# Handing out the y blocks of the second half in four parts a unit instead of one

## The chip, the cores and the metric

The kernel runs on one NeuronCore of a Trainium2 chip. The metric is the device time of one execution in microseconds (us), the median of several runs; less is better.

## The reference, cut to what matters

The reference has two layers on a 256 x 256 image of 128 channels. Layer 0 is a row attention (until about 1,655 us of the span). Layer 1 is a Fourier-operator block over 256 tokens (one token is a 256 x 128 plane): an attention whose value and projection are spectral convolutions, then two mixing layers, each a skip plus a spectral convolution over groups of four tokens, with instance norms. Cut to the part that the change touches:

```python
attn = fno_layer(attn, p_wr, p_wi, p_bias, p_sw, p_sb, (H, W))       # "y": attention-weighted tokens plus spectral image
attn = instance_norm(attn + tokens, attn_norm_w, attn_norm_b)
h0 = instance_norm(attn, norm2_w, norm2_b)                            # its statistics need all of y of those tokens
h1 = fno_layer(h0, mix_wr[0], mix_wi[0], ..., norm=True, act=True)    # first mixing layer: modes, then images
h2 = fno_layer(h1, mix_wr[1], mix_wi[1], ..., norm=True)              # second mixing layer
out = instance_norm(h2, mon_w, mon_b) + attn
```

The 256 tokens are worked on in two halves of 128 (half 0 and half 1)[...]. All data are float32.

## The kernel before

**Units of y.** `y_blocks(a, psum, lo, hi)` makes y of half `a` in units of 1,024 pixels, 32 units in all. A unit takes four PSUM banks (`yps`, one for each row residue `j`). For each `j`, TensorE adds two products of 128 x 256 (line 1351, over the two halves of the source tokens). After that come the products of `image` (line 1219, eight of 32 x 128 rows with the modes `gs`). Then VectorE writes the four banks out with a factor (line 1361, "eviction" below) and takes statistics of them (two `bn_stats`, line 1363). For half 1 the unit goes back to DRAM by a DMA that GpSimd issues (line 1365, tile `yt`, two buffers). The loads of unit `u + 2` (`xt`, three buffers, two DMAs of 512 KB on SyncE's queue, line 1017, and for every second unit four of `gs`, line 1248) are issued at the start of unit `u`.

**Banks.** PSUM is split between two sets of four banks, `bq` (tag q) and `br` (tag r). The units of half 1 use `br`, so a unit takes all of its set: the first product of the next unit waits for the eviction of the first bank.

**The mode chain of half 0.** While half 1's y is made, `first_modes(0)` works on the modes of the first mixing layer of half 0. Its steps are:

- `bn_aggr` of y's statistics (line 1451), then two chains of tiny VectorE operations, each with a square root on ScalarE (`rsqrt`, lines 35 to 43), that end in the tile `dg`;
- `rhops`, one product on TensorE (line 1468), its copy and the scaling of the modes `F` (lines 1471 to 1474);
- `mix_modes`: sixteen products `x0m` of 128 x 512 elements by VectorE or, every third one, GpSimd (line 1387, two buffers), each added into one of two banks by TensorE (`x0acc`, line 1400, identity as weights, 128 x 512). They are called step 0 to step 15 below;
- `mixed`: the copies and squares of the two banks (`x0Z`, `x0sq`, lines 1410 to 1416);
- four chunks of `synth_modes` (`g10gp`, 64 products each on TensorE, line 609; copies `g10gt`, line 617; DMAs `Gd`, line 622), and between them `norm`: the sums `x0ens` (line 1425), a third chain with a square root, then `x0rsp` (line 1438) and, after a product of it on VectorE (`bl`, line 1490), lines 1493 to 1508.

**Order.** The stages run in a `manual_schedule`: on every engine, SyncE included, instructions stand in the order in which the Python generators issue them, and each engine's queue is worked off in that order. `weave(main, side)` sets the order of the two chains. `main` yields a weight `t` after each of its steps. `weave` then takes parts of `side` until their own weights make up for it:

```python
for t in main:
    due += t
    while due > 0 and side is not None:
        u = next(side, None)
        ...
        due -= u
```

`y_blocks` yields 4.2 after each unit, so steps of the mode chain stand only between whole units. There are two such weaves: units 0 to 23 of half 1 with `first_modes(0)` (all of it), and units 24 to 31 with the first three yields of `second_modes(0)` (`f1ps` of its first two chunks, line 1629). Half 0 of y and the ends of both loops are run with `run`, which ignores the weights.

Of the kernel before, what the change touches and what calls it, by code (L numbers as in the profile page):

```python
# [22 lines left out]
def bc(ap, axis, n):  # L23

    a = ap.unsqueeze(axis)
    shape = list(a.shape)
    shape[axis] = n
    return a.to_broadcast(shape)
# [517 lines left out]
def layer1(tc, I, C, ident, x1d, upool, U, stats2, groups, out):  # L546
# [9 lines left out]
    with ExitStack() as ctx:  # L556
# [456 lines left out]
        def load_x1(a, u):  # L1013

            t = xp.tile([P, 2, NB // 2], FP, tag="xt", name=f"xt_{a}_{u}", bufs=3)
            for sc in range(2):
                nc.sync.dma_start(t[:, sc], x1v[:, sc, u * NB // 2 : (u + 1) * NB // 2])
            return t
# [188 lines left out]
        def by_turn(t):  # L1207

            return t.rearrange("p (n j w) -> p j n w", j=4, w=W)

        def rows_of(ps):
            return ps.rearrange("p (n w) -> p n w", w=W)

        def image(ps, gs, bs, rows=range(4)):

            for k, n in enumerate(rows):
                for j in range(4):
                    q = slice(32 * j, 32 * j + 32)
                    nc.tensor.matmul(  # L1219
                        ps[j][:, k * W : (k + 1) * W], gs[q, n, :], bs[q, :],  # L1220
                        start=False, stop=(k == len(rows) - 1),
                    )
# [16 lines left out]
        def load_modes(gs, Gd, b, tt=None):  # L1239
            for j in range(4):  # L1240
                q = slice(32 * j, 32 * j + 32)
                if tt is None:
                    nc.sync.dma_start(  # L1243
                        gs[q].rearrange("f n t -> f (n t)"),
                        Gd[:, j, 4 * b : 4 * b + 4, :].rearrange("f n t -> f (n t)"),
                    )
                else:
                    nc.sync.dma_start(gs[q], Gd[:, j, 4 * b : 4 * b + 4, tt])
# [78 lines left out]
        def y_blocks(a, psum, lo, hi, kept=16):  # L1327

            tt = slice(a * P, (a + 1) * P)
            gs = {}  # L1330

            def load(u):
                if (a, u) not in xts:
                    xts[a, u] = load_x1(a, u)
                if u % 2 == 0:
                    gs[u // 2] = xp.tile([P, 4, P], FP, tag="gs", name=f"gs_{a}_{u}", bufs=3)
                    load_modes(gs[u // 2], Gd0, u // 2, tt)

            load(lo)
            load(lo + 1)  # L1340
            yield 0.0
            for u in range(lo, hi):
                b, s = u // 2, u % 2
                if u + 2 < hi:
                    load(u + 2)
                xt = xts.pop((a, u))
                ps = [psum.pool.tile([P, 512], FP, tag=psum.tag, name=f"yps_{a}_{u}_{j}") for j in range(4)]
                ps = [z[:, 0:256] for z in ps]
                for j in range(4):
                    for sc in range(2):  # L1350
                        nc.tensor.matmul(  # L1351
                            rows_of(ps[j]), mpT[:, sc, tt], by_turn(xt[:, sc])[:, j],
                            start=(sc == 0), stop=False,
                        )
                image(ps, gs[b], bsy, range(2 * s, 2 * s + 2))
                if a == 0:
                    yt = blocks[:, b, s * HB : (s + 1) * HB]
                else:
                    yt = xp.tile([P, HB], FP, tag="yt", name=f"yt_{u}")
                for j in range(4):  # L1360
                    nc.vector.tensor_tensor(by_turn(yt)[:, j], rows_of(ps[j]), bc(rwb, 1, 2), ALU.mult)  # L1361
                for g in range(2):
                    nc.vector.bn_stats(ystat[:, a, 2 * u + g, :], yt[:, g * 512 : (g + 1) * 512])
                if a:
                    nc.gpsimd.dma_start(ydv[:, a, u * HB : (u + 1) * HB], yt)  # L1365
                yield 4.2

        def mix_modes(mk, acc, F, l, tag, cs):

# [443 lines left out]
        with tc.manual_schedule(engines=COMPUTE | {ENG.SP}):  # L1813
            with tc.tile_pool(name="psy", bufs=8, space=PSUM) as psy:
                run(y_blocks(0, Banks(psy, "y"), 0, 32))
# [6 lines left out]
            with yctx:  # L1822
                U1 = 24
                with tc.tile_pool(name="mp0", bufs=1) as wp:
                    y1 = y_blocks(1, br, 0, U1)
                    weave((2.4 * t for t in first_modes(0, wp, tiles(wp), bq, [(wp, "gt", 1)])), y1)
                    run(y1)
                with tc.tile_pool(name="hp0", bufs=2) as wp:
                    run(first_images(0, wp, xp, bq, br))
                with tc.tile_pool(name="mp1", bufs=1) as wp:  # L1830
                    y1 = y_blocks(1, br, U1, 32)
                    next(y1)
                    m0 = second_modes(
                        0, wp, tiles(wp), bq, [(xp, "xt", 3)], [(wp, "gt", 1)] * 3 + [(xp, "xt", 3)]
                    )
                    weave((2.4 * next(m0) for _ in range(3)), y1)
                    run(y1)
                    m1 = first_modes(
                        1, wp, Tiles(F=(xp, "yt", 2), f=(xp, "yt", 2), m=(xp, "gs", 3)), br, [(xp, "xt", 3)]
                    )  # L1840
                    next(m1)
                    for k, _ in enumerate(iter(lambda: next(m0), None)):
                        if k % 4 == 3:
                            next(m1)
                    for _ in m0:
                        next(m1, None)
                    o0 = output_0(bq)
                    next(o0)
                    y2 = wp.tile([P, NB], FP, tag="gt", name="y2_0", bufs=1)
                    nc.sync.dma_start(y2, ydv[:, 1, 0:NB])  # L1850
                    run(m1)
                    g2 = wp.tile([P, 4, P], FP, tag="m", name="gs2_1_0", bufs=2)
                    next(o0)
                    load_modes(g2, halves[1].Gd1, 0)
                    next(o0)
# [200 lines left out]
```

## Time and profile before

| | |
|---|---|
| time before, median of 3 runs | 2884.54 us (2880.02 to 2887.79) |
| profiled execution, its own time | 2878.79 us |
| its span, first to last instruction | 2877.0 us |
| TensorE (PE) busy in the span | 2643.1 us (92%) |
| VectorE (DVE) busy | 2004.2 us (70%) |
| units 0 to 23 of half 1, with `first_modes(0)` | about 2032 to 2190 us |
| of which `x0acc` and units 5 to 10 | about 2058 to 2110 us |
| units 24 to 31 of half 1 | about 2331 to 2385 us |

Times inside the profile are microseconds from the span's start. In the answers of the trace, a row of the timeline gives the start, the length, engine, line and operation, and in square brackets how long the engine was idle before it and what it waited for. A table of stretches gives the busy time in each, then the granted TensorE clock (1.00 is full), the share of the DMA engines and GB/s. TensorE runs each float32 product as two instructions, so a unit's eight products of line 1351 are 16 in the trace, and sixteen steps of `x0acc` are 32.

### The profile page before, as it was taken

Reading aid. Unit: us, or ns where it says so; the run is one execution under the profiler, and the core shown is the slowest. Engines: PE = TensorE matmul, PEld = TensorE weight load, DVE = VectorE, ACT = ScalarE, POOL = GpSimd, SP = SyncE. Lnnn points to the kernel's source line nnn. Section 1 sums busy time; section 2 is a strip of 40 time slices with the busy share of each in tenths; the row PEclk is TensorE's granted clock in tenths of the full one; section 3 lists DMA queues with packets and bytes.
Section 4 is the critical chain, followed back from the end, with each engine's and each line's share of the span. In section 5 each row is a group of like instructions: output and inputs, shape, how many; then the busy total and the mean of one; then the engine's idle time right before and its main releaser. Section 6 shows DMA issues by size and latency. Waiting matters only on the chain. (4 is left out here: it accounts for less than half of the span.)

```text
span 2877.0 us, 71481 instructions
## 1 busy us (share of the span) xinstructions
PE 2643.1 (92%) x29116; PEld 1935.1 (67%) x29116; DVE 2004.2 (70%) x3264; ACT 1488.4 (52%) x2847; POOL 1679.6 (58%) x1308
## 2 busy tenths in 40 slices
PE   7799999999999999999999989999889988799655
PEld 6677777777777777777777656778665555455533
DVE  7788888888888888888888854756645555365445
ACT  0477777777777777777777622200004611365132
POOL 0399999999999999999999900200114733111211
PEclk9999999999999999999999999999999999799865
DMA  9422222222222222222222101188879984798599
GB/s 369 166 67 67 67 67 67 67 67 67 68 67 67 67 67 67 67 67 67 67 67 67 47 22 54 34 276 274 281 243 312 311 304 134 253 363 306 187 360 339
DMA packets 246705, 430.12 MB, mean 149 GB/s; under 512 B 26278, under 2 KB 174201, under 8 KB 239976
## 3 DMA queue, kind: packets, MB, share of 16 engines
q1 hardware_dynamic: 206568, 335.34, 35.4%
q0 software_dynamic: 22912, 81.80, 7.4%
q10 hardware_dynamic: 16896, 8.39, 1.0%
q8 instruction: 231, 3.78, 0.6%
q14 instruction: 98, 0.80, 0.1%
HBM read 290.17 MB, written 135.27 MB: 148 GB/s over the span
## 5 line engine op out<-in xcount | busy, mean ns | idle before, releaser
L332 POOL TENSOR_TENSOR e<-e,b1T 128x1024 f32<-128x1024 f32 x256 | 606.1, 2367 | 164.6 <-PE u L381 90.3
L336 POOL TENSOR_TENSOR es<-e 128x512 f32<-128x512 f32 x512 | 639.6, 1270 | 20.1
L314 ACT ACTIVATE sc<-sc,b2T 128x512 f32<-128x512 f32 x512 | 339.0, 662 | 364.6 <-PE sc L305 356.2
L356 DVE RECIPROCAL av<-av 128x256 f32<-128x256 f32 x256 | 452.3, 1767 | 27.2 <-DVE og L355 1.4
L314 ACT ACTIVATE e<-sc,b2T 128x512 f32<-128x512 f32 x512 | 348.6, 681 | 0.0
L327 DVE TENSOR_TENSOR e<-sc,b1T 128x1024 f32<-128x1024 f32 x256 | 311.0, 1215 | 0.0
L305 PE MATMUL sc<-qkT 32*128 32x256 f32 x4096 | 293.4, 400 | 1.3 <-DVE e L327 1.3
L344 PE MATMUL av<-e,v 128*32 128x256 f32 x4096 | 274.7, 385 | 0.5 <-POOL e L332 0.5
L305 PEld LDWEIGHTS sc<-qkT 32*128 32x128 f32 x4096 | 185.1, 184 | 112.2 <-issue 97.7
L1351 PE MATMUL yps<-xt,mpT 128*128 128x256 f32 x1024 | 241.8, 389 | 19.4 <-DVE yt L1361 9.7
L355 DVE SCALAR_TENSOR_TENSOR og<-gate,av 128x256 f32<-128x256 f32 x256 | 107.7, 421 | 190.6 <-PE av L349 190.6
L1351 PEld LDWEIGHTS yps<-xt,mpT 128*128 128x128 f32 x1024 | 191.9, 192 | 56.7 <-DVE yt L1361 13.0
L1365 POOL DMA_DIRECT2D yd<-yt x32 | 17.7, 555 | 340.8 <-DVE yt L1361 340.8
L360 POOL TENSOR_TENSOR x<-xt,bo 128x256 f32<-128x256 f32 x256 | 187.7, 734 | 0.0
L279 PE MATMUL qk<-xnT,wT_wq 128*128 128x256 f32 x512 | 179.5, 432 | 1.7 <-ACT xnT L271 1.7
L285 PEld LDWEIGHTS gv<-wT_wv,kvT 128*128 128x128 f32 x1024 | 155.0, 192 | 13.3
L349 PE MATMUL av<-es,ones 128*32 128x256 f32 x2048 | 157.5, 379 | 2.5 <-POOL es L336 2.5
L366 PE MATMUL wo<-wT_wo,og 128*128 128x128 f32 x1024 | 156.8, 276 | 2.7 <-DVE og L357 2.7
L344 PEld LDWEIGHTS av<-e,v 128*32 128x32 f32 x4096 | 107.0, 109 | 76.1 <-POOL e L332 1.0
L381 PE MATMUL u<-adft,x 128*128 128x129 f32 x1024 | 156.4, 275 | 0.0
L285 PE MATMUL gv<-wT_wv,kvT 128*128 128x128 f32 x1024 | 156.0, 275 | 0.0
L1718 ACT ACTIVATE blocks<-h2ps,col 128x512 f32<-128x512 f32 x128 | 89.0, 779 | 129.4 <-PE h2ps L1219 129.4
(546 smaller groups left out, 5282.8 us busy)
## 6 DMA issues: line engine op xcount, KB each, us to landing
xt<-x1d SPq DMA_DIRECT2D x128, 512.0 KB, 5.9
xb<-in_x_dram SPq DMA_DIRECT2D x32, 1024.0 KB, 7.8
xt<-in_x_dram SPq DMA_DIRECT2D x128, 256.0 KB, 2.7
kt<-in_L_conv_kv_x_dram SPq DMA_DIRECT2D x128, 256.0 KB
x1d<-x SPq DMA_DIRECT2D x256, 128.0 KB, 2.3
y<-yd SPq DMA_DIRECT2D x62, 512.0 KB, 8.9
gs<-Gd SPq DMA_DIRECT2D x384, 64.0 KB, 5.1
yd<-yt POOLq DMA_DIRECT2D x32, 512.0 KB, 6.3
```

The costliest lines, as they stand in the source:

```text
L279: nc.tensor.matmul(ps[:, 0:256], wT["wq"], xnT, start=True, stop=True)
L285: nc.tensor.matmul(ps[:, 256 + c * P : 256 + (c + 1) * P], kvT[:, c * P : (c + 1) * P], wT["wv"], start=True, stop=True,)
L305: nc.tensor.matmul(sc[h // 2][:, h % 2, c * 256 : (c + 1) * 256], qkT[p, 256 + c * P : 256 + (c + 1) * P], qkT[p, 0:256], start=True, stop ...
L314: nc.scalar.activation(r["e"][1][:, :, c, :] if hp else z, z, AF.Exp, bias=b2T[:, c, s : s + 1])
L327: nc.vector.tensor_tensor(r["e"][0].rearrange("p h c q -> p (h c q)"), r.pop("sc").rearrange("p h x -> p (h x)"), b1T[:, 0:2].rearrange("p ...
L332: nc.gpsimd.tensor_tensor(e1, e1, b1T[:, 2:4].rearrange("p h c q -> p (h c q)"), ALU.mult)
L336: nc.gpsimd.tensor_tensor(r["es"][hp], e[:, :, 0, :], e[:, :, 1, :], ALU.add)
L344: nc.tensor.matmul(ps[hd, 0:256], r["v"][:, c, hd], r["e"][h // 2][:, h % 2, c, :], start=(c == 0), stop=(c == 1),)
L349: nc.tensor.matmul(ps[32 * h : 32 * h + 32, 256:512], self.ones, r["es"][h // 2][:, h % 2, :], start=True, stop=True,)
L356: nc.vector.reciprocal(rd, rd)
L360: nc.gpsimd.tensor_tensor(r["x1"], r["x"], bc(self.bo, 1, 2), ALU.add)
L1351: nc.tensor.matmul(rows_of(ps[j]), mpT[:, sc, tt], by_turn(xt[:, sc])[:, j], start=(sc == 0), stop=False,)
```

## The change

A unit of y now yields three more times, after the products of `j` = 0, 1 and 2, with 0.86 each, and 1.62 instead of 4.2 at its end; the sum is the same. The generator's own instructions and their order among themselves do not change, nor do buffers or banks. In the two weaves, steps of the mode chain can now stand after each pair of products of a unit.

```diff
--- before.py
+++ after.py
@@ -1352,6 +1352,8 @@
                             rows_of(ps[j]), mpT[:, sc, tt], by_turn(xt[:, sc])[:, j],
                             start=(sc == 0), stop=False,
                         )
+                    if j < 3:
+                        yield 0.86
                 image(ps, gs[b], bsy, range(2 * s, 2 * s + 2))
                 if a == 0:
                     yt = blocks[:, b, s * HB : (s + 1) * HB]
@@ -1363,7 +1365,7 @@
                     nc.vector.bn_stats(ystat[:, a, 2 * u + g, :], yt[:, g * 512 : (g + 1) * 512])
                 if a:
                     nc.gpsimd.dma_start(ydv[:, a, u * HB : (u + 1) * HB], yt)
-                yield 4.2
+                yield 1.62
 
         def mix_modes(mk, acc, F, l, tag, cs):
```

In the order of the two built programs, these instructions of the mode chains change place (unit numbers are of half 1; a step of `x0acc` on TensorE, its product `x0m` on VectorE or GpSimd):

| what | before | after |
|---|---|---|
| first chain with a square root (VectorE) | after the eviction of unit 0 | ahead of it |
| second chain (VectorE) | after the eviction of unit 1 | ahead of it |
| `rhops` (TensorE) | after unit 3 | in unit 3, after `j` = 0 |
| steps 0 and 1 of `x0acc` | after unit 5 | in unit 5, after `j` = 0 and `j` = 1 |
| step 2 | after unit 5 | after unit 5 |
| steps 3 to 14 | three after each of units 6 to 9 | in each of units 6 to 9 one after `j` = 0, one after `j` = 1 (unit 6) or `j` = 2 (7 to 9), one after the unit |
| step 15 | after unit 10 | in unit 10, after `j` = 0 |
| VectorE's copy `x0Z` | after the eviction of unit 10 | ahead of it |
| `x0ens` | after unit 12 | in unit 12, after `j` = 1 |
| `x0rsp`, lines 1493 to 1508, third `g10gp` | after unit 15 | in unit 15, after `j` = 1; on VectorE ahead of its eviction, on GpSimd ahead of its DMA |
| first `f1ps` of `second_modes(0)` | after unit 27 | in unit 27, after `j` = 2; its copy ahead of the eviction |

On SyncE's queue nothing changes place; half 0 of y is unchanged.

## The prediction

> **What bounds the stage now.** I read the page first for the whole (TensorE is busy 92% of the span), then the waits of TensorE between 2030 and 2170 us, where units 0 to 18 of half 1 run with the mode chain of half 0, then the timelines of TensorE, VectorE and GpSimd there, then tables of stretches for clock and DMA. The change moves no instruction outside half 1's two weaves, so the rest can only shift as a block.
>
> The waits of TensorE in that window:
> ```profile
> PE x0acc L1400 <- POOL x0m L1387: 7.7, 5, 1.6
> PE yps L1351 <- DVE yt L1361: 5.3, 8, 1.4
> PE g10gp L609 <- ACT x0sq L1416: 2.9, 1, 2.9
> PE x0rsp L1493 <- DVE bl L1490: 2.6, 1, 2.6
> ```
> The columns are us in total, times, longest. Five waits of 1.5 us are the third step of each group of three; two long single waits follow. TensorE's timeline shows one full period of such a unit (start, length, work; the idle before in brackets):
> ```profile
> 2070.68 1.98 PE L1400 MATMUL x0acc<-x0m,ident 128*128 128x512 f32 x4
> 2074.21 1.12 PE L1400 MATMUL x0acc<-x0m,ident 128*128 128x512 f32 x2 [1.55 <-POOL x0m L1387]
> 2075.17 3.62 PE L1351 MATMUL yps<-xt,mpT 128*128 128x256 f32 x16
> 2078.72 0.73 PE L1219 MATMUL yps<-bsy,gs 32*128 32x128 f32 x16
> 2079.38 1.98 PE L1400 MATMUL x0acc<-x0m,ident 128*128 128x512 f32 x4
> ```
> The period is 2079.38 - 2070.68 = 8.70 us. Start to start, products take 3.55, the image 0.66, a step 0.95; full work is 3.55 + 0.66 + 3 x 0.95 = 7.06. The reader should see that 1.6 us per unit is idle. Its cause is in VectorE's and GpSimd's timelines:
> ```profile
> 2070.77 1.42 DVE L1361 TENSOR_TENSOR yt<-yps,rwb 128x256 f32<-128x256 f32 x4 [3.40 <-PE yps L1219]
> 2072.22 1.28 DVE L1363 BATCH_NORM_STATS2 ystat<-yt 128x6 f32<-128x512 f32 x2
> 2073.42 1.29 DVE L1387 TENSOR_TENSOR x0m<-F,mixwi 128x512 f32<-128x512 f32 x1
> 2073.10 1.06 POOL L1387 TENSOR_TENSOR x0m<-F,mixwn 128x512 f32<-128x512 f32 x1
> ```
> GpSimd's product stands behind the DMA of `yt`, VectorE's behind eviction and statistics: 2.66 us from the start of an eviction to the next `x0m`.
>
> The clock, before, in and after the two long waits:
> ```profile
> 2101.30:2109.50 8.20, 5.30 (x35) 1.00 0.62 212
> 2109.50:2113.10 3.60, 3.56 (x128) 0.53 0.27 106
> 2142.70:2145.40 2.70, 2.32 (x12) 0.69 1.05 391
> 2145.40:2149.40 4.00, 4.00 (x130) 0.50 0.52 183
> 2149.40:2154.30 4.90, 4.90 (x41) 0.88 0.57 154
> ```
> The column after TensorE's busy time and count is the granted clock. A `g10gp` chunk takes 2.03 us at full clock (2128.41 to 2130.44) and 3.60 here.
>
> [...]after the waits of 1.43 to 1.55 us in this stage the clock stayed at 1.00, after 2.03 (at 2456 us), 2.19 (2194 and 2495), 2.36 (2406), 2.58 and 2.94 us it was 0.50 to 0.56; one wait of 2.72 (2725 us) went without. [...]`x0m` on VectorE takes 0.69 us alone and 1.29 beside GpSimd's. [...]2160 to 2180 us shows 345 to 350 with units at their shortest period, 4.88 us.
>
> **The change part by part.** I count lag, after minus before, along TensorE's order.
>
> *Start, units 0 to 4: a loss.* The first chain takes 3.16 us from its first operation to the free VectorE (2039.10 to 2042.26, ScalarE's table load of 1.28 in it). Before, it ran behind unit 0's eviction and half hid under unit 1. Now it runs first, from the end of `bn_aggr` at 2035.24, so the eviction moves from 2036.44 to 2038.4, and unit 1 from 2036.92 to 2038.9: lag +1.96, and a wait of 2.45 us (wait A). The second chain (2.62 us) moves ahead of unit 1's eviction in the same way, but as unit 2 had waited 1.43 us and unit 3 0.89 before, it costs nothing more: by the same sums units 2 and 3 start at 2044.15 and 2049.0, lag +1.4 and +1.0. `rhops` (0.57) covered the 0.50 us in which a unit waits for the first eviction; inside unit 3 it covers nothing. Lag +1.6 at unit 5.
>
> *Unit 5: a loss.* Step 0 stands after `j` = 0, but its product on VectorE is 2.66 + 0.68 us behind the start of unit 4's eviction: ready 2062.3, against `j` = 0 done at 2060.3. Wait B, 2.0 us. At step 2's end the lag is +2.1 (2068.6 against 2066.48).
>
> *Units 6 to 9: the gain meant.* A step at the unit's end waits for GpSimd's product, whose buffer comes free at the step after `j` = 0, 2.8 us into the period; it is done 1.06 us later, ahead of 7. The VectorE product, ready between 3.5 and 4.1 us into the period, is wanted at 3.8 in unit 6 (0.1 to 0.3 us of wait) and at 4.6 in units 7 to 9. So periods of 7.15 and three times 7.06 for 8.69 and three times 8.70: -1.5 and -4.9. Lag -4.3.
>
> *Unit 10 to `g10gp`.* Before, 2101.27 to 2109.54 = 8.27 us. Now step 15 is in the unit, and `x0Z` and `x0sq` are done 2 us ahead of the unit's end: 3.55 + 0.95 + 0.66 = 5.16. Lag -7.4. Without the 2.94 us wait the chunk runs at full clock, 2.03 for 3.60: -9.0.
>
> *Unit 12.* `x0ens` (1.80) covered a 0.50 us turn and no longer does: -8.5.
>
> *Units 15 and 16.* Before, from the end of unit 15 (2139.62): `x0rsp`, a wait of 2.58 for `bl` behind eviction and statistics, four products of line 1504 (1.83 where 0.95 would do), a chunk of 3.93, and unit 16 0.58 slow. Now `x0rsp` comes after `j` = 1, when unit 14's statistics have just ended (2.75 us after its image), so `bl` is at once; two waits of about 0.4 and 0.6 stay, and unit 16 waits 0.5 for its bank. By the same sums the third chunk starts at 2140.0 on unit 15's old clock and unit 16 at 2144.9 for 2149.37: -4.5, with its slow 0.58 -5.0. Lag -13.5. Behind this on GpSimd, two `Gd` DMAs pass one of `yt`; that costs 1.5 us on a queue idle two thirds of the time. The copies `g10gt` end some 2 us ahead of the eviction that they now precede.
>
> *Unit 27.* `f1ps` (1.88) no longer covers the turn: +0.5. SyncE's load of the next `YT` is released 1.5 us sooner, which no wait of TensorE asks for. Lag -13.0.
>
> *Clock at waits A and B.* The trace of before does not have them. Lower bound: nothing, as after 1.55 us. Upper: 2.5 each, as after the 2.58 us wait (1.9 in the chunk, 0.6 in unit 16). I take a drop for both, since 2.0 to 2.6 us dropped the clock five times in five, at 1.9 us each, of which 0.4 at A hides behind the second chain: +3.4. The extra yields are Python's and cost nothing on the chip.
>
> Sum: -13.0 + 3.4 = **-9.6 us**. The profiled execution took 2878.79, so it would be 2869.2. The median of the runs is 5.75 above it; carrying the saving over, 2884.54 - 9.6 = **2875 us**. About 0.3% (8.7 us) is what a measurement can tell from no change, so this forecast stands just past that line.
>
> **Rivals.**
> - *No drop of the clock at A and B*: -13.0, 2871.5. [...]Against: five drops in five.
> - *Steps come late*: the product of VectorE is 1.3 us late in units 6 to 9, if [...]the statistics run long. 4 x 1.3 = 5.2 of the gain is gone: -4.4, 2880.
> - *DMA takes back what unit 15 gave*: from unit 14 on, 7.35 MB move in 25.8 us before and would have 20.8, 353 GB/s, at the 345 to 350 seen. Against: loads land 5.4 us (6.4 at most) after issue and have some 9. It would give -9.6 + 5.0 = -4.6, 2880.
> - *Half clock stays (slower)*: [...]units 6 to 10 run at half rate: their work of 33 us takes 67 for 43.1 before, +24, plus 5.5 of lag at the start, less 6 later: about +23, 2908. [...]Against: units with 1.55 us idle held 1.00, and unit 5 behind B has no gap.
>
> That the order does not change is no rival: the built program's order shows it.
>
> **How the numbers follow.** Forecast 0.53, no drop 0.16, late steps 0.14, DMA 0.12, half clock 0.05. The forecast passes 0.3% in two thirds of its spread (+-2.5 us): 0.35; no drop nearly always: 0.15; the others 0.04. Faster 0.54, slower 0.05, same 0.41. The range goes from no drop less 3 us of spread between runs (2868) to the two partial cases plus 3 (2883).
>
> **What would show it.** Right: the five waits on GpSimd gone, the period of units 7 to 9 near 7.1; `g10gp` directly behind unit 10 at clock 1.0; the wait before line 1493 below 0.6 us; a wait near 2.4 us before unit 1 and one near 2.0 before step 0, each with clock 0.5 behind it. Wrong: steps 4, 7, 10 and 13 waiting for VectorE, TensorE waiting for `xt` in units 14 to 23, or clock 0.5 through units 6 to 10.

## The result and the profile after

The changed kernel takes 2874.25 us (median of 22 runs, 2869.46 to 2879.43). The kernel before, in runs beside it, takes 2882.3 us (22 runs, 2875.28 to 2888.59). The ratio is 0.9972, with a 95% interval of 0.9965 to 0.9978. That is 8.1 us less, between 6.3 and 10.1. The forecast was 2875.0.

One table of a single stretch shows most of it. The stretch runs from the first product of unit 0 of half 1 to the first product of the stage behind unit 23 (`ups`). Its columns are the bounds, the length, then the busy time and the number of instructions of TensorE, its weight loads, VectorE, ScalarE and GpSimd, then clock, DMA share and GB/s. First the kernel before, then the changed one:

```profile
2032.05:2190.15 158.10, 136.92 (x1345) 105.17 (x1345) 89.04 (x205) 10.16 (x17) 24.25 (x36) 0.97 0.80 269
```

```profile
2036.55:2184.26 147.71, 133.39 (x1345) 102.79 (x1345) 86.20 (x205) 10.16 (x17) 25.39 (x36) 0.99 0.84 287
```

The same 1,345 products now need 147.71 us for 158.10, so 10.39 less. TensorE's idle time went from 158.10 - 136.92 = 21.18 to 147.71 - 133.39 = 14.32, so 6.86 of it is idle time. The other 3.53 is busy time: the same products ran less at half clock (mean clock 0.99 for 0.97). The repeats of both kernels, told of below, differ by 158.13 - 150.42 = 7.7 us in this stretch; the runs' 8.1 lies between the two. Length times rate gives nearly the same bytes in both (158.10 x 269 and 147.71 x 287, within 0.4%), so GB/s rose from 269 to 287.

The two spans differ by less, 2877.0 - 2872.2 = 4.8 us. Unit 0 began 4.50 us later in the execution after, in code that the change does not touch. The experiments come back to it.

The waits of TensorE between 2034 and 2174 us of the changed kernel (us in total, times, longest; the lines of the code stand two lower than before):

```profile
PE yps L1351 <- DVE yt L1363: 10.3, 12, 2.5
PE x0acc L1402 <- DVE x0m L1389: 1.8, 1, 1.8
...
PE x0rsp L1506 <- DVE turned L1501: 0.4, 1, 0.4
PE x0rsp L1495 <- DVE bl L1492: 0.4, 1, 0.4
```

The five waits on GpSimd (7.7 us) and the 2.94 us before `g10gp` are gone, and the wait for `bl` is 0.38 for 2.58. In their place stand the waits that the prediction called A (2.50, in the first line) and B (1.77). The first line also holds one that it did not have: 2.30 us before unit 16. Waits for an eviction rose from 5.3 to 10.3 us.

One period of a unit, here unit 8, in TensorE's timeline:

```profile
2079.91 1.12 PE L1402 MATMUL x0acc<-x0m,ident 128*128 128x512 f32 x2
2080.87 1.03 PE L1351 MATMUL yps<-xt,mpT 128*128 128x256 f32 x4
2081.74 1.02 PE L1402 MATMUL x0acc<-x0m,ident 128*128 128x512 f32 x2
2082.59 1.89 PE L1351 MATMUL yps<-xt,mpT 128*128 128x256 f32 x8
2084.32 1.02 PE L1402 MATMUL x0acc<-x0m,ident 128*128 128x512 f32 x2
2085.18 1.03 PE L1351 MATMUL yps<-xt,mpT 128*128 128x256 f32 x4
2086.14 0.73 PE L1219 MATMUL yps<-bsy,gs 32*128 32x128 f32 x16
2086.79 1.13 PE L1402 MATMUL x0acc<-x0m,ident 128*128 128x512 f32 x2
```

From 2079.91 to 2086.79 is 6.88 us, where it was 8.70, and no row has idle time ahead of it. A step between two products of a unit costs 0.86 start to start; behind an image it costs 0.96. That is why the period is still 0.18 shorter than the 7.06 of the forecast.

The reason is on GpSimd. Two rows of its timeline in that period, with the idle before each row in brackets:

```profile
2081.71 0.60 POOL L1367 DMA_DIRECT2D yd<-yt  x1 [4.39 <-DVE yt L1363]
2082.92 1.32 POOL L1389 TENSOR_TENSOR x0m<-F,mixwr 128x512 f32<-128x512 f32 x1 [0.61 <-PE x0acc L1402]
```

GpSimd's product still stands behind the DMA of `yt` in the queue, but the DMA is no longer what it waits for: its buffer comes free only behind the step after `j` = 0, 0.61 us after the DMA. The product is done at 2084.24, and the step that needs it comes at the unit's end, at 2086.79. So its delay is hidden now.

### The profile page after: what moved, and what is told of

The parts are those of the page before. It is cut to its first block, busy times and chain, and to the rows that moved or that the text cites. A ratio compares the mean times of both kernels' runs of the same rounds, so it can differ in the third digit from the quotient of the medians.

```text
span 2872.2 us, 71485 instructions
## 1 busy us (share of the span) xinstructions
PE 2643.2 (92%) x29116; PEld 1932.7 (67%) x29116; DVE 2004.7 (70%) x3264; ACT 1488.2 (52%) x2847; POOL 1683.2 (59%) x1308
## 5 line engine op out<-in xcount | busy, mean ns | idle before, releaser
L1351 PE MATMUL yps<-xt,mpT 128*128 128x256 f32 x1024 | 247.9, 394 | 20.8 <-DVE yt L1363 13.9
L291 DVE COPY v<-gv 128x256 f32<-128x256 f32 x256 | 108.6, 424 | 68.5 <-PE gv L289 68.5
```

Source lines behind the costliest of these rows:

```text
L1351: nc.tensor.matmul(rows_of(ps[j]), mpT[:, sc, tt], by_turn(xt[:, sc])[:, j], start=(sc == 0), stop=False,)
```

## The experiments

"The stretch" below is the one of the table: 158.10 us before, 147.71 after, each in one execution. Unit starts are counted from unit 0 of half 1. Ratios are to the kernel before, run beside each kernel.

**Parts apart: units 6 and up only.** The first six units keep their order from before.

```diff
-                    if j < 3:
+                    if j < 3 and u >= 6:
                         yield 0.86
-                yield 1.62
+                yield 1.62 if u >= 6 else 4.2
```

> Units 0 to 5 of half 1 whole as before, parts from unit 6 on. The stretch is from the first product of unit 0 of half 1 to the first product of the next stage: 158.1 us before, 147.7 with the change. Theory (each place gives its own amount: start a loss, steps a gain, unit 15 a gain): the wait of 2.5 us before unit 1 and its half clock are gone, unit 6 begins 34.4 us after unit 0 as before (37.4 with the change), so the stretch is 144.7 us and the median some 3 us below the change's. Rival (the early square roots are what lets the steps start, so the start's loss is the price of the gain): the steps come as much later, 147.7.

Measured: ratio 0.9953 (0.9938 to 0.9969), 2870.61 us for 2884.27. The stretch is 145.42. Unit 6 starts at 34.43 as before (37.41 after), so the loss at the start is gone. The stretch shows 2.29 of the 2.98 us won there; two waits take back some: an issue gap of 1.01 in unit 14, where the change has 0.45, and 1.46 for `yt` at unit 22. Unit 16 waited only 0.50 here, though the order from unit 6 on is that of the change.

**The other part: units 0 to 5 only** (`u < 6` in both places).

> Parts in units 0 to 5 of half 1 only, whole from unit 6 on: the start alone. Theory: wait of 2.4 to 2.5 us before unit 1 and a wait near 1.8 us before step 0, unit 6 begins 37.4 us after unit 0; the five-fold wait of 1.5 us on GpSimd is back in units 6 to 9; stretch 161.1 us, 3 us slower than before, the median too. Rival (the gain comes from the mode chain being ahead of the units): the stretch is below 158.1.

Measured: ratio 1.0005 (0.9997 to 1.0014), no gain. The stretch is 162.26 where 161.1 was expected, with unit 6 at 37.42. Two rows of its timeline show what the start adds and what is left undone:

```profile
2067.42 1.13 PE L1402 MATMUL x0acc<-x0m,ident 128*128 128x512 f32 x2 [1.77 <-DVE x0m L1389]
...
2089.91 1.13 PE L1402 MATMUL x0acc<-x0m,ident 128*128 128x512 f32 x2 [1.55 <-POOL x0m L1389]
```

Wait B comes with the first units alone, and the wait on GpSimd is back in the later ones. The first six units are a cost of 3.0 us in the trace (the runs say 0.9 less to 4.0 more) and hold no part of the gain.

**Units 6 to 10 only** (`6 <= u <= 10`).

> Parts in units 6 to 10 only: the steps of the sum alone. Theory: periods of 6.9 us in units 6 to 9, no wait before the first g10gp chunk and that at full clock, later units as before with the 2.6 us wait and the slow third chunk: stretch 146.1 us, 12 us under before. Rival (half of the gain hangs on unit 15): 150 us or more.

Measured: ratio 0.9957 (0.994 to 0.9974), 2872.01 us. The stretch is 144.14 where 146.1 was expected: these five units alone bring 13.96 us of it, more than the whole change. The long wait ahead of the third `g10gp` chunk is back in TensorE's timeline:

```profile
2132.38 0.38 PE L1495 MATMUL x0rsp<-col,blk 128*128 128x1 f32 x2 [2.58 <-DVE bl L1492]
```

Half clock came with it, as a table of the chunk's stretch shows (the clock is the third number from the end):

```profile
2134.50:2138.00 3.50, 3.50 (x128) 3.34 (x128) 0.12 (x1) 0.02 (x1) 0.00 (x0) 0.54 0.70 233
```

Even so its ratio is that of the kernel with units 6 and up, which has unit 15 rearranged too. So the runs show no worth of unit 15's part as it stands.

**Unit 15 only** (`u == 15`).

> Parts in unit 15 only. Theory: the 2.6 us wait before line 1493 becomes two of 0.4 and the third chunk runs at full clock, but its copies wait for the DMA of the second chunk (one buffer) and unit 15's eviction behind them lets unit 16 wait 2 us: net -2.7, stretch 155.4 us. Rival (the copies' wait was chance of one execution): unit 16 waits 0.5 us, stretch 153 us.

Measured: ratio 0.9997 (0.9985 to 1.0008), stretch 157.71. Unit 15 to unit 17 takes 17.79 us for 20.97, so 3.2 are won where the edit is. But units 11 and 13, in an order that is the same as before, together with unit 12 took 2.8 us more (81.13 to 101.26, before 81.09 to 98.39). The clock behind the first `g10gp` chunk shows a part of it, in the kernel before and in this one:

```profile
2113.20:2118.00 4.80, 4.31 (x34) 3.43 (x32) 1.76 (x4) 1.07 (x2) 1.52 (x2) 1.00 0.54 145
```

```profile
2114.60:2120.60 6.00, 5.54 (x40) 4.31 (x32) 1.73 (x4) 1.07 (x2) 1.51 (x2) 0.80 0.63 170
```

Both follow the same wait of 2.94 us. In one, unit 11 ran at full clock; in the other, half clock lasted into it. It came again in unit 13 (0.71), with no wait ahead of it but the 16 products of `x0ens`, which are one column wide.

The wait of 2 us that was expected at unit 16 did not come; it is 0.50, as the rival had it. The third chunk ran at half clock (3.7 us for 2.0), so its copies came later, and they waited for the chunk's products and not for a DMA:

```profile
2147.99 1.29 DVE L617 COPY g10gt<-g10gp 128x512 f32<-128x512 f32 x2 [3.52 <-PE g10gp L609]
```

The interval (4.3 us less to 2.3 more) does not decide whether unit 15 alone brings anything over many runs.

**The cause of the five waits.** The order of before, with the DMA of `yt` issued from ScalarE's queue:

```diff
-                    nc.gpsimd.dma_start(ydv[:, a, u * HB : (u + 1) * HB], yt)
+                    nc.scalar.dma_start(ydv[:, a, u * HB : (u + 1) * HB], yt)
```

> The kernel before (whole units), with the DMA of yt issued from ScalarE's queue instead of GpSimd's. Theory (the third step of a group is late because GpSimd's product stands behind a DMA that waits for the eviction): the product starts when its buffer is free, 0.95 us into the group, and is done 1.3 us sooner; the five waits of 1.5 us shrink to 0.2, the stretch goes from 158.1 to 151.3 us, the rest as before. Rival (the product is late for its buffer[...]): waits and stretch stay, 158 us.

Measured: ratio 0.998 (0.9969 to 0.999), 2880.51 us for 2885.57, stretch 155.24 where 151.3 was expected. Its waits between 2034 and 2174 us:

```profile
PE g10gp L609 <- ACT x0sq L1416: 2.9, 1, 2.9
PE x0rsp L1493 <- DVE bl L1490: 2.6, 1, 2.6
PE x0acc L1400 <- POOL x0m L1387: 1.5, 4, 0.4
```

The waits on GpSimd fell from 1.55 to at most 0.39, and unit 10 started at 63.44 for 69.22, 5.8 us sooner. GpSimd's product now starts when its buffer comes free, not when `yt` is written:

```profile
2071.18 1.05 POOL L1387 TENSOR_TENSOR x0m<-F,mixwn 128x512 f32<-128x512 f32 x1 [6.43 <-PE x0acc L1400]
```

So the queued DMA was the cause of these waits, as the prediction read it. The stretch kept only 2.9 of the 5.8: units 11 to 13 took 2.8 us more than in before (75.36 to 95.45), with the clock at 0.81 and 0.71 in units 11 and 13.

**The wait at unit 16.** In the changed kernel, VectorE stood still ahead of unit 15's eviction. Its timeline (start, length, operation, idle before), then TensorE's first row of unit 16:

```profile
2136.50 0.17 DVE L1510 COPY turn<-x0rsp 128x8 f32<-128x8 f32 x1 [0.74 <-PE x0rsp L1506]
2142.13 1.29 DVE L617 COPY g10gt<-g10gp 128x512 f32<-128x512 f32 x2 [5.46 <-DMA Gd<-g10gt]
2143.33 1.41 DVE L1363 TENSOR_TENSOR yt<-yps,rwb 128x256 f32<-128x256 f32 x4
```

```profile
2143.80 3.72 PE L1351 MATMUL yps<-xt,mpT 128*128 128x256 f32 x16 [2.30 <-DVE yt L1363]
```

The third chunk's copies write `g10gt`, for which `first_modes(0)` has one buffer. They waited until 2142.1 for the DMAs `Gd` that read it for the second chunk, issued at about 2129, and the eviction stood behind them: unit 15's last product was done at 2141.50, and VectorE came to it at 2143.33, after the copies, as the program has them. To test it, the third chunk is set one unit later, behind an extra yield, with the weights' sum unchanged:

```diff
-                yield 2.4
+                yield 1.2 if c == 2 else 2.4
...
                     nc.vector.tensor_copy(h.turn, ps[:, 260:268])
+                    yield 1.2
```

> The change, with one more yield behind line 1510 (1.2, taken from the chunk's 2.4): the third chunk comes after unit 15 instead of into it, so its copies stand behind unit 15's eviction on VectorE; the small products of lines 1440 to 1506 stay in unit 15. Theory (unit 16 waited for an eviction behind copies that wait for a DMA): the 2.3 us wait of unit 16 is gone, stretch 145.3 us for 147.7, median 2 us below the change. Rival (DMA is the bound there, and a wait would only move): a wait of 2 us for xt or yd elsewhere in units 16 to 18, stretch 147.7.

Measured: ratio 0.996 (0.9946 to 0.9973), stretch 144.65. Unit 16 no longer waits, and starts at 102.82 for 107.25. From unit 6 on, that is 66.59 for 69.84, so 3.25 sooner. But the trouble moved on, to the fourth chunk's copies and then unit 18, where 1.32 of the 3.25 are left:

```profile
2149.88 1.29 DVE L617 COPY g10gt<-g10gp 128x512 f32<-128x512 f32 x2 [4.33 <-DMA Gd<-g10gt]
```

```profile
2151.55 3.72 PE L1351 MATMUL yps<-xt,mpT 128*128 128x256 f32 x16 [2.43 <-DVE yt L1363]
```

The chain holds (copies behind the one buffer's DMA, eviction behind the copies), and two chunks near each other can bring it back. It need not come: with units 6 and up, and with unit 15 only, the third chunk stands in unit 15 as in the change and unit 16 waited 0.50. The copies came 12.2 and 11.1 us after the first `Gd` DMA of the second chunk was issued, and no DMA held them; in the two executions of the change they were held until 13.5 and 11.6 us after it. Why these DMAs take longer at one time than at another is not shown. The interval of the ratio overlaps the change's, so the gain of this edit over the change is not shown by the runs.

The first units of the same execution show something else. After wait A of 2.50 us its clock, beside that of the kernel with units 0 to 5 only (same order, same wait), that one first:

```profile
2043.00:2045.00 2.00, 2.00 (x5) 1.64 (x6) 1.97 (x5) 0.00 (x0) 0.76 (x1) 0.50 0.57 231
```

```profile
2042.50:2044.50 2.00, 2.00 (x9) 1.78 (x10) 1.97 (x5) 0.00 (x0) 0.77 (x1) 1.00 0.51 207
```

The same wait gave half clock in one and none in the other; the end of this section says why.

**Both mends: units 6 and up, and the third chunk set apart** (the two diffs together).

> Parts from unit 6 on only, and the third chunk after unit 15 as in the split. If both theories hold their amounts add: 147.7 - 3.0 - 2.4 = 142.3 us of stretch, 15.8 under before, median some 13 us below before. If the DMA comes to bind in units 14 to 23, it stays at 144 to 145.

Measured: ratio 0.9942 (0.9928 to 0.9956), 2870.08 us for 2885.57, stretch 142.83. This interval lies wholly below that of the change, so this version beats both kernels. Unit 18 waited 0.50, though its chunks stand in the same places as with the third chunk set apart alone.

**The same, with the DMA of `yt` on ScalarE.**

> Parts from unit 6 on, third chunk after unit 15, and the DMA of yt from ScalarE's queue: a candidate for the best. Theory: the one group that is left whole (steps 0 to 2 after unit 5) loses its wait of 1.5 us to 0.4, the rest is as with parts from 6 and the split: stretch 141.7 us for 142.8. Rival (a DMA on ScalarE's queue holds up its copies and squares while it waits for the eviction): stretch 143 or more, a wait before g10gp.

Measured: ratio 0.9948 (0.9931 to 0.9965), not to be told from the one before. Its stretch is 144.85 where 141.7 was expected. The first group's wait went (unit 6 at 33.34), but unit 20 waited 1.77 with half clock behind it: units 19 to 21 took 3.0 us more than with both mends alone, which is the miss of the expectation. Behind the stretch, the first wait of the next stage on ScalarE rose from 2.19 to 4.45 (4.44 with the DMA alone moved).

**Both kernels once more, unchanged.** The doubt was whether the first profile of before had been a lucky one.

> The kernel before, unchanged, for a second profiled execution. Theory ([...]the first profile was a lucky one behind the 2.9 us wait): same waits to 0.1 us, but units 11 and 13 slow (clock 0.7 to 0.8), stretch about 161 us for 158.1. Rival (the other kernels' slow units 11 and 13 come from their edits): 158.1 again.

> The change, unchanged, for a second profiled execution. Theory: the waits of 2.5 us before unit 1 and 1.8 us before step 0 again; half clock after the first in some executions only; the wait of unit 16 for the copies of the third chunk again, between 1 and 2.5 us; stretch 146.5 to 149 us. Rival (the wait of unit 16 was one late DMA): unit 16 waits 0.5 us.

Measured: the stretch of before is 158.13, within 0.03 of the first, so a single lucky profile is not the explanation: units 11 and 13 were fast again, as the rival had it. That of after is 150.42, where 146.5 to 149 was expected. In that execution, unit 16 waited only 0.97, but at unit 20 the wait for `yt` was 1.38, and unit 21 waited in its midst for its load, with the clock at 0.68 from 2170.50 to 2174.00:

```profile
2170.50 4.98 PE L1351 MATMUL yps<-xt,mpT 128*128 128x256 f32 x14 [2.34 <-DMA xt<-x1d]
```

**The later start of unit 0.** At about 1857 us every execution has the same wait of 2.13 us (`g0gp`). From there to `fyps`, identical code took 26.1 to 26.2 us in five executions (both of before among them), 28.7 to 28.8 in four, and 30.4 to 30.5 in three (both of after among them); in the execution after, the clock behind that wait was 0.50 to 0.70 for 1.00 before. If that loss belonged to the kernel, the one with units 0 to 5 only, which had 30.4 too, would lose it on top of its longer stretch: 4.2 + 4.2 = 8.4 us. Its runs measured 1.4 more (0.9 less to 4.0 more). So it does not look like the kernel's own, and the clock's record, which comes next, shows what it is.

**Where a wait falls.** In each of the twelve traces, every change of the granted clock lies on a grid of 3.413 us, to within 0.002 us; between 1850 and 2196 us, half clock lasts 3.41, 6.83 or 10.24 us each time. The grid lies differently against the program in each execution, so that the same wait lies whole between two of its lines (a window, below) or is split over two windows. Here is the window with most of wait A in the changed kernel, then the two windows that share wait A in the kernel with the third chunk set apart:

```profile
2039.84:2043.25 3.41, 1.09 (x18) 0.56 (x17) 1.57 (x10) 1.49 (x2) 0.00 (x0) 1.00 0.60 168
```

```profile
2037.11:2040.53 3.42, 2.86 (x27) 2.13 (x25) 1.82 (x2) 1.48 (x2) 0.00 (x0) 1.00 0.75 174
2040.53:2043.94 3.41, 1.47 (x7) 1.32 (x8) 3.10 (x13) 0.00 (x1) 0.23 (x1) 1.00 0.76 296
```

In the first, TensorE was busy for 0.32 of the window, and half clock followed. In the other two it was busy for 0.84 and 0.43, and none followed. Between 1850 and 2196 us, the twelve traces hold 22 windows at full clock with a busy share under 0.40, and half clock followed all of them. From 0.40 to 0.50 it followed 7 of 9, from 0.50 to 0.60 none of 31. Above that it followed 8 of 1,103, of which seven hold products of `x0ens` or `x0rsp` that are one or two columns wide.

This settles the later start of unit 0. The wait of 2.13 us is split over two windows (busy 0.51 to 0.54 and 0.62 to 0.64) in the five executions with 26.1 to 26.2 us; it lies in one window (0.37) in the seven others, with half clock for 6.83 us in four of them and 10.24 us in three. It also bears on units 11 and 13: the 2.94 us lie in one window (busy 0.14) in both executions of before and are split in the three others, of which the kernel with unit 15 only (0.38 and 0.75) has the order of before up to there. Half clock ended 3.5 us behind the start of the first chunk in the two, 4.8 to 6.0 us in the three.

## Why the prediction was right

The forecast said -9.6 us; the runs say -8.1 (-6.3 to -10.1), and the stretch -10.39, with 0.8 lost at unit 27. The points of lag along TensorE's order, after minus before, with the +3.4 of the clock in the forecast from unit 6 on:

| point | forecast | measured |
|---|---|---|
| unit 1 | +1.96, wait 2.45 | +2.01, wait 2.50 |
| unit 2 | +2.9 | +2.65 |
| unit 6 | +5.5 | +2.98 |
| periods of units 6 to 9 | 7.15, then 7.06 | 6.91, 6.89, 6.88, 6.88 |
| unit 10 | -0.9 | -4.25 |
| first `g10gp` | -4.0 | -7.46 |
| unit 11 | -5.6 | -9.03 |
| unit 13 | -5.1 | -8.48 |
| third chunk | -10.5 | -13.55 |
| unit 16 | -9.6 | -10.07 |
| `ups` | -10.1 | -10.39 |
| unit 27 to 28 | +0.5 | +0.77 |

The changed kernel was 3.4 us further ahead at unit 10 than forecast, and only 0.5 at unit 16.

**Right.** Wait A came to 0.05 us as worked out, and GpSimd's product was hidden as described. From unit 10 to the first chunk 3.2 us were won (3.1 forecast), over the chunk 1.6 (1.6), and 0.55 was lost at unit 12's turn (0.5). Without its wait, the first chunk ran at full clock. A stretch over each of the places shows the clock after wait A, after wait B and in that chunk:

```profile
2043.40:2045.40 2.00, 1.97 (x5) 1.61 (x6) 1.97 (x5) 0.00 (x0) 0.73 (x1) 0.50 0.53 215
...
2068.00:2072.00 4.00, 4.00 (x15) 2.79 (x16) 1.08 (x2) 0.00 (x0) 1.04 (x1) 1.00 0.42 170
...
2106.58:2108.60 2.02, 2.02 (x132) 1.85 (x128) 1.90 (x5) 0.00 (x1) 0.21 (x1) 1.00 0.76 180
```

**Mis-sized: the term "clock at waits A and B", +3.4.** After A half clock cost 1.58 us in the products and 1.25 in the lag (1.5 forecast). After B it cost nothing (1.9 forecast): B was 1.77 long, not 2.0, and the clock stayed at 1.00. The reason given, "2.0 to 2.6 us dropped the clock five times in five", put B just inside a range it fell short of, and the count was not whole: the trace of before has a wait of 2.14 us at 1857.54 with the clock at 1.00 behind it. What failed is pricing by length alone. B was split over two windows (busy 0.54 and 0.80) and kept full clock, while the wait of 1.77 us at unit 20 of the kernel with both mends and the DMA on ScalarE lay in one (0.48) and lost it.

**Mis-sized: the periods.** 6.9 for 7.1 us: a step between products was priced like one behind an image. With four units that is 0.8 us of gain not forecast.

**The step that failed: "the copies `g10gt` end some 2 us ahead of the eviction that they now precede".** In both executions of the change they ended after it was due, because the second chunk's DMAs still held the one buffer. So of the 5.0 us forecast for units 15 and 16, 2.67 came in the first execution (20.97 to 18.30), and 2.30 is the new wait. The prediction counted the two `Gd` DMAs only as time on GpSimd's queue, not as the hold on the buffer that the next chunk's copies need. With units 6 and up, and with unit 15 only, the hold ended in time, but there the third chunk ran at half clock, and 3.1 and 3.2 of the 5.0 came. This miss and the two sizes above nearly cancel: 3.4 us better than forecast at unit 10, 2.3 worse in units 15 and 16. That the sum came out at -10.4 for -10.1 is partly luck.

**The rivals.** "DMA takes back what unit 15 gave" was counted at 12%. It was not what the first execution showed, but the second one showed a part of it (2.34 and 1.38 us of waits in units 20 and 21). "Steps come late" and "half clock stays" did not come: units 6 to 9 had no wait, and clock 1.00.

## What to carry to other kernels

Ask of each step moved forward what it needs that is still held: a buffer with one copy ties it to the DMA of the step before it, and everything behind it in an engine's queue waits too (here VectorE stood still for 5.46 us ahead of the copies, and unit 16 waited 2.30 for the eviction behind them). Weave side work into a main unit only where the trace shows a wait to fill: here units 6 to 10 brought the gain, units 0 to 5 cost 3 us in the trace, and unit 15 shifted a wait. Price a wait with what the clock may add behind it, as a span from nothing to its measured worst: here half clock came behind all 22 windows of 3.41 us that were less than 0.40 busy, behind 7 of 9 from 0.40 to 0.50 and none of 31 from 0.50 to 0.60, and where the windows lie differs from one execution to the next.

## What the runs showed of the hardware that was not expected

- The same idle time gives different clocks, by where it lies on the clock's grid of 3.413 us. After 2.50 us half clock came three times and stayed away once; after 2.13 us it came seven times and stayed away five times, and what followed took 26.2, 28.7 or 30.4 us. Waits of 1.77 us gave both outcomes too: the clock stayed at 1.00 behind wait B of the changed kernel, and unit 20 of the kernel with both mends and the DMA on ScalarE took 5.41 us for its products, where units 21 and 22, at full clock, take 3.72.
- Half clock can come with no wait: in three executions (units 0 to 5 only, unit 15 only, the DMA of `yt` on ScalarE) it slowed unit 13 by 1.7 us, with the clock at 0.71 to 0.72 there, behind a window of 3.41 us in which TensorE counts as fully busy but which holds the 16 one-column products of `x0ens`.
- A DMA on GpSimd's queue that waited for its data held up the product behind it: TensorE waited up to 1.55 us per unit for that product, at most 0.39 with the DMA on ScalarE's queue.
- Of two `x0m` products that overlap, the one that begins second is the longer, in all nine pairs of before and after. Before, VectorE's began 0.32 to 0.40 us behind GpSimd's and took 1.22 to 1.30, where one alone takes 0.69; in unit 8 of the changed kernel GpSimd's began 0.27 behind (2082.92 for 2082.65) and took 1.32, where one alone takes 1.04, VectorE's 0.67.
